# Two graph-attention layers on one core: aggregates scaled on VectorE, weights begun one product sooner, no sums of h in one aggregate

## The chip, the cores and the metric

The kernel runs on one core of a Trainium2 chip. A core has five engines with queues of their own: TensorE (PE in the profile, and PEld for its weight loads), VectorE (DVE), ScalarE (ACT), GpSimd (POOL) and SyncE (SP). Here POOL and SP mostly issue DMA transfers. The metric is the device time of one execution in microseconds. All data is fp32 apart from the masks.

## The reference

There are N = 2708 nodes with 1024 features, and a matrix `adj` of which only `adj > 0` counts. Both layers are residual and work on a normalized input:

```python
h = relu(layernorm(x));  e = relu((h@Wf + bf) @ (h@Wg + bg).T)      # layer l=0
x = x + softmax(where(adj > 0, e, -9e15)) @ (h@W + bW)
h = relu(layernorm(x));  z = h@W1;  e = leaky_relu(z@a1 + (z@a2).T, 0.2)   # layer l=1
x = x + relu(softmax(where(adj > 0, e, -9e15)) @ z)
```

The softmax runs over all nodes for each node, so each layer multiplies a 2708 x 2708 matrix of weights with a 2708 x 1024 matrix. The kernel applies the weights to h first and W afterwards, as softmax(e) @ (h @ W) = (softmax(e) @ h) @ W.

## The kernel before

**Panels.** The nodes for which attention is computed are cut into five panels, p = 0 to 4, of 576, 576, 532, 512 and 512 columns (`width[p]`; h is half of it). The nodes over which the softmax sums are 20 tiles of 128 rows, taken as ten pairs q (NQ = 10), and two left-over tiles, MONO and TINY.

**Products.** Each large product is cut two by two and done with seven products of half size instead of eight (Strassen's scheme in Winograd's form): M1, M5, M2, M6, M7, M3, M4, with sums of operands made beforehand and sums of results made as the products leave PSUM. The tile pool `psum` has eight banks. `accumulate` (line 647) gives four banks to each accumulator: x takes M1 and M2, y takes M5 and M3, z takes M6 and M7, v takes M4. The order in the aggregates that concern us is M1, M5, M2, M6, M3, M7, M4. After a product its four banks are emptied ("evicted"), by DVE or ACT.

**Stages.** In l=0, panel p goes through `scores`, a softmax, `aggregate` (line 885: weights times h) and `project` (line 1202: times W, plus the residual). Around the panel 3 to panel 4 border they interleave; the last two stages of l=0 are the aggregate of panel 4, its fifth, and the projection of panel 4, which goes pair by pair (`by_pair`) and fetches its weight tiles twice. That projection also makes the last rows of h for l=1. In l=1 the scores come from two vectors, so there are only weight steps, `aggregate` for panel 0, `aggregate_quartered` (line 1039) for panels 1 to 4, and a projection after each. In the quartered aggregate each of the seven products is itself done by seven products on quarters (`product`, line 1052), the last of which, `left_out`, is emitted in the next product's time.

**Sums of h.** The quartered aggregates need sums of quarters of h for every product m and every group k of four tiles: 35 steps (`put_quarters`, line 392, tile `hq`). One step is two loads issued by POOL, four DVE instructions of 256 columns, and two stores issued by POOL, 1 MB of traffic in all. They wait in a list `lazy`. From the panel 4 on their buffers come from the pool of slots (54 buffers), two for each step.

**Weight steps of l=1.** `take_shifts(p)` (line 1781) first empties the list `later`, then takes the column maxima (five transposes on PE into two PSUM banks, reductions on DVE) and works out two columns of shifts. `take_weights(p)` (line 1785) spreads them over all partitions (ten transposes on PE) and puts 24 steps at the head of `later`: 22 tiles and two that only lag behind. A step is an ACT instruction, two DVE instructions, an exponential on ACT, and an addition into `sm` on DVE; each has a mask load on SP of its own. `sm` collects the sums by which the aggregate is divided.

**Who is served when.** Between the matmuls the program calls `behind(us)` (line 211). It adds `us` to a credit, capped at twice `us`, and emits work from `later` while the credit is positive, each item at its own price: 2.1 for a weight step, 1.7 for a sum of h. Only where `later` is empty and `spare[0]` is true are items of `lazy` emitted. In an `aggregate` of ten pairs there are four calls per product, three within it and one after its eviction, at a rate of 3.0 in l=0 and 4.0 in l=1. Loads of the next items (`ahead`) are emitted ahead of them. `exps_until` and `quarters_until` emit what must be there, whatever the credit.

**Order on an engine.** What the program emits is a priority, not yet an order: the tile framework's scheduler orders each engine's queue at compile time by when it thinks that an instruction can run and a buffer is free, earlier emitted ones first. [...]

**Scaling.** An aggregate G (two halves `G[0]`, `G[1]`, each of four chunks of columns) is multiplied by the inverse of the sums: `inverse_sums` (line 858) adds `sm` over partitions on PE and takes reciprocals on DVE. In the quartered aggregate the quadrants become final in the order (0,lo) with M2, (1,hi) with M7, (0,hi) with M3 and (1,lo) with M4. `scale` (line 1092) multiplies `G[0]` and the quadrant (1,hi) on POOL after M3, and a DVE instruction at the end multiplies (1,lo). The projection's first product reads `G[0]`.

Of the kernel before, what the change touches and what calls it, by code (L numbers as in the profile page):

```python
# [12 lines left out]
OP = mybir.AluOpType  # L13
# [5 lines left out]
P = 128  # L19
# [6 lines left out]
M1, M5, M6, M7, M3, M2, M4 = range(7)  # L26
# [31 lines left out]
def kernel(  # L58
# [19 lines left out]
    nc = InOrder(tc)  # L78
    N, D = x.shape
    NC = D // P  # L80
    NH = NC // 2
# [3 lines left out]
    NP = N // W  # L85
# [110 lines left out]
    spare, from_slots = [False], [False]  # L196
# [437 lines left out]
    for name, gs in (("pick_lo", (0, 1)), ("pick_hi", (0, 2, 3))):  # L634
        t = consts.tile([P, P], FP, name=name)
# [403 lines left out]
    def aggregate_quartered(p, S, sm, of_right, then={}, fine=1.2):  # L1039

        w = width[p]
        h = w // 2
        hb = h // 2
        lo, hi = slice(0, h), slice(h, w)
        G = both("gT")
        quad = lambda e, s: G[e].rearrange("p (c i) -> p c i", c=NH)[:, :, s]
        make, inner_right = of_right["make"], of_right["right"]
        lasts = {}  # L1050

        def product(m, n, ps, start):
            quarters_until(m)
            if (m, 0) not in lasts:
                for i, of in enumerate((hr_d[:, m, :, :, NK - 1].rearrange("p h f c -> p (h f) c"), hs2_d[:, m, :, NK - 1])):
                    lasts[m, i] = stream("hl2", (P, 4, WH))
                    load(lasts[m, i], of)
            t = stream("hc2", (P, NK - 1, WH))
            raw = n in (M1, M2, M4)
            i = {M1: 0, M2: 1, M4: 3, M6: 0, M3: 1, M7: 2, M5: 3}[n]  # L1060
            load(t, hr_d[:, m, i // 2, i % 2, :NK - 1] if raw else hs2_d[:, m, i, :NK - 1])
            last = lasts[m, int(not raw)][:, i]
            for k in range(NK):
                for d in range(2):
                    lhs = t[:, k] if k < NK - 1 else last
                    nc.tensor.matmul(ps[:, d], lhs[:, d * P:(d + 1) * P], inner_right(m, n, k),  # L1066
                                     start=(start and k == 0 and d == 0), stop=(k == NK - 1), skip_group_check=True)
            behind(fine)

        def bank2(name):  # L1070
            return bank(name)[:, :2 * hb].rearrange("p (d i) -> p d i", d=2)

        def left_over(banks, e, s, fresh):

            two = stream("hl", (P, W + 2 * P))
            load(two, hgl_d[1][:, e])
            cols = lambda b: slice(s.start + b * hb, s.start + (b + 1) * hb)
            for (a, b), ps in banks.items():
                for d in range(2):
                    c = 2 * a + d  # L1080
                    nc.tensor.matmul(ps[:, d], two[:, c * P:(c + 1) * P], S[MONO][:, cols(b)],
                                     start=((a, b) in fresh and d == 0), stop=False, skip_group_check=True)
            for d in range(2):
                for (a, b), ps in banks.items():
                    g = slice(B32 * (2 * a + b), B32 * (2 * a + b) + NY)
                    nc.tensor.matmul(ps[:, d], two[g, W + d * P:W + (d + 1) * P], S[TINY][g, cols(b)], start=False, stop=True,
                                     skip_group_check=True)

        inverse = []
        by = lambda s, c, k: inverse[0][:, s].rearrange("p (o i) -> p o i", o=1).to_broadcast([P, c, k])  # L1090

        def scale():
            for t, s, k in ((quad(0, slice(0, w)), slice(0, w), w), (quad(1, hi), hi, h)):
                nc.gpsimd.tensor_tensor(t, t, by(s, NH, k), OP.mult)

        place = {M1: [(1, lo)], M5: [(0, hi)], M2: [(0, lo)], M6: [(0, hi), (1, lo)], M7: [(1, hi), (1, lo)], M3: [(0, hi)],
                 M4: [(1, lo)]}
        direct = {M1: (0, lo), M5: (0, hi)}
        more_of = {M2: (0, lo), M3: (0, hi), M4: (1, lo)}

        def into_place(m, V, r):
            for e, s in place[m]:
                o = quad(e, s)[:, 2 * r:2 * r + 2]
                if m == M1:
                    nc.scalar.copy(o, V[r])
                elif m == M5:
                    add(o, o, quad(0, lo)[:, 2 * r:2 * r + 2])
                else:
                    add(o, V[r], o)

        def corner():

            four = {(a, b): bank2("gu") for a in range(2) for b in range(2)}
            left_over(four, 1, hi, four)
            for (a, b), ps in four.items():
                at = lambda e: quad(e, slice(h + b * hb, h + (b + 1) * hb))[:, 2 * a:2 * a + 2]
                add(at(1), ps, at(0))

        def with_second():
            exps_until(2 * NQ + 2 + LAG)  # L1120
            make(M2)

        before_next = {M1: lambda: make(M5), M5: with_second, M2: lambda: (of_right["fourth"](), make(M6)), M6: lambda: make(M7),
                       M7: lambda: make(M3), M3: lambda: make(M4)}
        left_out = None
        for m in BY_QUARTERS:
            V = [quad(*direct[m])[:, 2 * r:2 * r + 2] for r in range(2)] if m in direct else [v[:, :, :h] for v in in_pairs("V")]
            c11, c12 = (V[0][:, :, b * hb:(b + 1) * hb] for b in range(2))
            c21, c22 = (V[1][:, :, b * hb:(b + 1) * hb] for b in range(2))
            X = bank2("gx")  # L1130
            product(m, M1, X, True)
            nc.scalar.copy(c21, X)
            if m == M1:
                of_right["fifth"]()
            if left_out:
                left_out()
            Z = bank2("gz")
            product(m, M6, Z, True)
            add(c12, Z, c21)
            Y = bank2("gy")  # L1140
            product(m, M5, Y, True)
            add(c22, Y, c21)
            if m == M7:
                corner()
            if m in before_next:
                before_next[m]()
            product(m, M2, X, False)
            if m not in more_of:
                nc.scalar.copy(c11, X)
            product(m, M7, Z, False)  # L1150
            add(c22, Z, c22)
            product(m, M3, Y, False)
            if m in more_of:
                U = bank2("gu")
                left_over({(0, 0): X, (0, 1): Y, (1, 0): Z, (1, 1): U}, *more_of[m], [(1, 1)])
                nc.scalar.copy(c11, X)
            add(c12, Y, c12)
            if m in more_of:
                add(c22, U, c22)
            into_place(m, V, 0)  # L1160

            def left_out(m=m, V=V, Z=Z, c21=c21):
                product(m, M4, Z, False)
                add(c21, Z, c21)
                into_place(m, V, 1)
                if m == M3:
                    scale()
            if m == M5:
                of_right["second"]()
            if m == M6:  # L1170
                inverse.append(inverse_sums(p, sm))
            if m in then:
                then[m]()
        left_out()
        o = quad(1, lo)
        nc.vector.tensor_tensor(o, o, by(lo, NH, h), OP.mult)
        return [t.rearrange("p (c i) -> p c i", c=NH) for t in G]

    w_in = [w0, w1]
# [486 lines left out]
    for p in range(NP):  # L1666
# [15 lines left out]
        then = {M4: lambda: sums_until(NQ), M5: prepare_W} if p == 0 else {}  # L1682
        ahead[0] = 1 if p == 0 else 2
        if p == NP - 2:
            then[M2] = lambda: first_masks(NP - 1, 0)
            then[M6] = lambda: first_masks(NP - 1, 1)
            then[M7] = lambda: first_masks(NP - 1, 2)
        spare[0], from_slots[0] = p > 0, p == NP - 1
        G[p] = aggregate(0, p, S, got["sm"], then)
        spare[0] = False  # L1690
        if p == 0:
# [89 lines left out]
    def take_shifts(p):  # L1781
        flush()
        got["zm"] = shifts1(p)

    def take_weights(p):
        got["P"] = weights1(p, *got["zm"])
# [3 lines left out]
    for p in range(NP):  # L1790
        S, sm = got["P"]
        then = {}
        if p + 1 < NP:
            then = dict(zip((M2, M6) if p else (M3, M7), (lambda p=p: take_shifts(p + 1), lambda p=p: take_weights(p + 1))))
        spare[0] = p == 0
        g = aggregate_quartered(p, S, sm, next_right, then, fine=1.0) if p else aggregate(1, p, S, sm, then, rate=4.0)
        hooks = {}
        if p + 1 < NP:
            next_right = quarters_of(p + 1, got["P"][0])
            hooks = {M7: next_right["first"]}  # L1800
        project(1, p, g, finish1(p), hooks, by_pair=(p == NP - 1), rate=1.7)
# [29 lines left out]
```

## Time and profile before

| What | Value |
|---|---|
| Median of 14 runs | 3126.07 us (3116.37 to 3129.79) |
| The profiled execution: its time, its span | 3127.64 us, 3125.9 us |
| Granted TensorE clock, mean | 0.984 |
| Busy: PE, DVE, POOL, ACT | 3016.2, 2067.7, 536.3, 463.0 us |
| PE busy in aggregate of panel 4, l=0 (1947 to 2083) | 133.91 of 136 us |
| PE busy in its projection (2083 to 2162) | 56.85 of 79 us, DMA share 1.00 |
| PE busy in aggregate 0 of l=1 (2162 to 2314) | 152 of 152 us |
| PE busy in aggregate 1 of l=1 (2350 to 2520) | 158.60 of 170 us |
| hq instructions on DVE | 28 in 1947 to 2083, 28 in 2162 to 2314 |

A line of the timeline holds the start and the length in us, the engine, the line of the kernel (L45 is the helper through which DVE and ACT instructions are issued), the operation, the tiles written and read, and the number of merged instructions. A bracket at its end is the time that the engine stood idle before it, and what ended the wait. "PEclk" and the granted clock are shares of full speed. "DMA share" is the mean busy share of the 16 DMA engines.

### The profile page before, as it was taken

The page shows a single profiled execution, that of the slowest core. Times are in us where ns is not written, and L with a number is a line of the kernel's source. Part 1 is how long each engine was busy: PE and PEld are TensorE (multiplying, and loading weights), DVE is VectorE, ACT ScalarE, POOL GpSimd, SP SyncE. Part 2 cuts the span into 40 slices and gives each one's busy share as a digit, 9 for nine tenths or more (in the row PEclk, how much of TensorE's full clock was granted, in tenths as well). Part 3 has the DMA queues.
Part 4 walks back from the last instruction along what each step waited for, and adds up shares of the span by engine and source line. Part 5 has one row for each costly group of instructions (what it writes and reads, how often), then busy time and mean ns, then how long its engine had stood idle before and what let it go on. Part 6 is the DMA issues. An engine that isn't in the chain of part 4 may idle for free.

```text
span 3125.9 us, 41677 instructions
## 1 busy us (share of the span) xinstructions
PE 3016.2 (96%) x14630; PEld 2314.1 (74%) x14630; DVE 2067.7 (66%) x4587; ACT 463.0 (15%) x817; POOL 536.3 (17%) x794
## 2 busy tenths in 40 slices
PE   8998999999999999999999999988999999999998
PEld 4576777657877588876888885864767959779694
DVE  5776692776742687527873478657777767777853
ACT  3420020000200101000020002103131121212200
POOL 1421111310112110123111101041211020120202
PEclk9999999999999999999999999998999999999999
DMA  6999967988466796768957677598857768777886
GB/s 230 291 270 257 310 243 261 297 264 243 152 231 161 231 250 211 244 165 254 287 176 249 177 218 246 195 319 291 288 172 246 243 208 298 256 274 272 268 290 247
DMA packets 448576, 764.69 MB, mean 245 GB/s; under 512 B 175776, under 2 KB 262592, under 8 KB 448368
## 3 DMA queue, kind: packets, MB, share of 16 engines
q1 hardware_dynamic: 393008, 598.31, 60.6%
q0 software_dynamic: 55360, 163.73, 15.9%
q8 instruction: 116, 1.90, 0.2%
q14 instruction: 92, 0.75, 0.1%
HBM read 627.95 MB, written 133.91 MB: 244 GB/s over the span
## 4 chain that ended last, share of the span: by engine, by line
PE 70%; DVE 13%; DMA 7%; issue 6%; SPq 2%; POOL 1%; ACT 1%; POOLq 0%; DVEq 0%; ACTq 0%
PE sz L1377 6%; PE gx L661 6%; PE gy L661 6%; PE gz L661 5%; PE gz L1066 5%; PE sx L1377 4%; PE sy L1377 4%; PE pz L1266 4%; PE px L1266 4%; PE py L1266 3%; PE gv L661 3%; PE M_ps L574 3%; PE gy L1066 3%; PE gx L1066 3%; PE qx L661 2%
## 5 line engine op out<-in xcount | busy, mean ns | idle before, releaser
L1377 PE MATMUL sz<-B,As 128*128 128x288 f32 (+2 forms) x1200 | 292.8, 393 | 9.5 <-DVE st L45 8.8
L1377 PEld LDWEIGHTS sz<-B,As 128*128 128x128 f32 x1200 | 228.3, 191 | 59.1 <-DVE st L45 12.7
L1377 PE MATMUL sx<-B,As 128*128 128x288 f32 (+2 forms) x800 | 203.3, 398 | 13.2 <-DMA As<-hs_d 10.1
L1377 PE MATMUL sy<-B,As 128*128 128x288 f32 (+2 forms) x800 | 199.1, 392 | 1.0 <-DMA As<-hs_d 1.0
L661 PE MATMUL gz<-Sa,hc 128*128 128x288 f32 (+2 forms) x800 | 188.1, 396 | 6.0 <-DMA hc<-hg_d 6.0
L1377 PEld LDWEIGHTS sx<-B,As 128*128 128x128 f32 x800 | 153.8, 193 | 47.4 <-issue 6.5
L661 PEld LDWEIGHTS gz<-Sa,hc 128*128 128x128 f32 x800 | 153.3, 192 | 39.0 <-DMA hc<-hg_d 6.4
L1066 PE MATMUL gz<-quarter,hc 128*128 128x128 f32 (+2 forms) x1344 | 170.2, 280 | 6.5 <-DVE gT L45 5.1
L1377 PEld LDWEIGHTS sy<-B,As 128*128 128x128 f32 x800 | 151.9, 190 | 31.7 <-ACT x L45 1.4
L1066 PEld LDWEIGHTS gz<-quarter,hc 128*128 128x128 f32 x1344 | 161.7, 192 | 8.9 <-DVE gT L45 6.5
L1266 PE MATMUL pz<-w,ps 128*128 128x512 f32 x320 | 145.2, 605 | 8.0 <-DVE pt L45 7.0
L1266 PE MATMUL py<-w,ps 128*128 128x512 f32 x320 | 142.5, 595 | 1.9 <-DMA w<-in_L_gnn_W_dram 1.9
L1266 PE MATMUL px<-w,gT 128*128 128x512 f32 x320 | 141.0, 593 | 0.0
L143 POOL DMA_DIRECT2D out_dram<-x_res x180 | 89.0, 500 | 256.6 <-DVE x_res L45 248.2
L143 POOL DMA_DIRECT2D mk_d<-mask x55 | 35.8, 651 | 533.3 <-DVE mask L45 526.9
L1266 PEld LDWEIGHTS pz<-w,ps 128*128 128x128 f32 x320 | 61.3, 194 | 86.9 <-issue 72.2
L1266 PEld LDWEIGHTS py<-w,ps 128*128 128x128 f32 x320 | 60.5, 190 | 77.9 <-issue 72.6
L574 PE MATMUL M_ps<-wgT,wfT 128*128 128x512 f32 x256 | 111.8, 593 | 1.6 <-ACT hsT L45 1.6
L1266 PEld LDWEIGHTS px<-w,gT 128*128 128x128 f32 x320 | 60.3, 190 | 71.0 <-issue 69.0
L661 PE MATMUL gy<-T,hc 128*128 128x288 f32 (+2 forms) x480 | 111.6, 394 | 0.0
L661 PEld LDWEIGHTS gy<-T,hc 128*128 128x128 f32 x480 | 91.4, 190 | 19.3
L977 POOL TENSOR_TENSOR gT<-gT,rr 128x2304 f32<-128x2304 f32 (+5 forms) x12 | 44.4, 3701 | 353.4 <-DVE rr L45 160.9
(378 smaller groups left out, 5864.4 us busy)
## 6 DMA issues: line engine op xcount, KB each, us to landing
hc<-hg_d SPq DMA_DIRECT2D x175, 512.0 KB
As<-hs_d SPq DMA_DIRECT2D x150, 512.0 KB
hc<-hr_d SPq DMA_DIRECT2D x119, 512.0 KB
hc<-hs_d SPq DMA_DIRECT2D x112, 512.0 KB
w<-wt_d SPq DMA_DIRECT2D x96, 512.0 KB
w<-in_L_gnn_W_dram SPq DMA_DIRECT2D x72, 512.0 KB
md<-md_d SPq DMA_DIRECT2D x56, 512.0 KB
adj_i<-in_adj_dram SPq DMA_DIRECT2D x200, 128.0 KB
```

The source lines that it names most:

```text
L143: nc.gpsimd.dma_start(a, b)
L574: nc.tensor.matmul(ps, wfT[a][c // NH][:, c % NH, :], wgT[b][c], start=(c == 0), stop=(c == NC - 1))
L661: nc.tensor.matmul(ps[d], left(m, k, d), right(m, k), start=(start and k == 0), stop=(k == K - 1), skip_group_check=True)
L977: nc.gpsimd.tensor_tensor(of(e, s), of(e, s), by(s, k), OP.mult)
L1066: nc.tensor.matmul(ps[:, d], lhs[:, d * P:(d + 1) * P], inner_right(m, n, k), start=(start and k == 0 and d == 0), stop=(k == NK - 1), ski ...
L1266: nc.tensor.matmul(ps, left[i][m][:, k, :], w_[k], start=(start and k == 0), stop=(k == NH - 1), skip_group_check=True)
L1377: nc.tensor.matmul(ps[:n, :h], lefts[q][:, i % 2, c, :n], B[m][c // 2][:, c % 2, :h], start=(start and c == 0), stop=(c == NH - 1), skip_g ...
```

## The change

1. In the quartered aggregates the scaling moves from POOL to DVE. After each of M2, M7, M3 and M4 the finished quadrant is multiplied in two parts, the first two chunks as soon as they are in place and the other two after the product's `left_out`. For that the inverse of the sums is made after M5 instead of after M6. POOL's two instructions and the single DVE instruction at the end go.
2. In l=1, panel 0, `take_shifts(1)` runs after M6 instead of after M3, and `take_weights(1)` after M3 instead of after M7.
3. In the aggregate of panel 4 of l=0 (the first layer's fifth), `spare[0]` is false, so no sums of h are emitted there. Those that are left come in aggregate 0 of l=1, where `spare[0]` is true as before.

```diff
         inverse = []
-        by = lambda s, c, k: inverse[0][:, s].rearrange("p (o i) -> p o i", o=1).to_broadcast([P, c, k])
-
-        def scale():
-            for t, s, k in ((quad(0, slice(0, w)), slice(0, w), w), (quad(1, hi), hi, h)):
-                nc.gpsimd.tensor_tensor(t, t, by(s, NH, k), OP.mult)
+        done_with = {M2: (0, lo), M7: (1, hi), M3: (0, hi), M4: (1, lo)}
+
+        def scale(m, r):
+            if m in done_with:
+                e, s = done_with[m]
+                o = quad(e, s)[:, 2 * r:2 * r + 2]
+                nc.vector.tensor_tensor(o, o, inverse[0][:, s].rearrange("p (o i) -> p o i", o=1).to_broadcast([P, 2, h]), OP.mult)
...
             into_place(m, V, 0)
+            scale(m, 0)
 
             def left_out(m=m, V=V, Z=Z, c21=c21):
                 product(m, M4, Z, False)
                 add(c21, Z, c21)
                 into_place(m, V, 1)
-                if m == M3:
-                    scale()
+                scale(m, 1)
             if m == M5:
                 of_right["second"]()
-            if m == M6:
+            if m == M5:
                 inverse.append(inverse_sums(p, sm))
             if m in then:
                 then[m]()
         left_out()
-        o = quad(1, lo)
-        nc.vector.tensor_tensor(o, o, by(lo, NH, h), OP.mult)
         return [t.rearrange("p (c i) -> p c i", c=NH) for t in G]
...
-        spare[0], from_slots[0] = p > 0, p == NP - 1
+        spare[0], from_slots[0] = 0 < p < NP - 1, p == NP - 1
         G[p] = aggregate(0, p, S, got["sm"], then)
...
-            then = dict(zip((M2, M6) if p else (M3, M7), (lambda p=p: take_shifts(p + 1), lambda p=p: take_weights(p + 1))))
+            then = dict(zip((M2, M6) if p else (M6, M3), (lambda p=p: take_shifts(p + 1), lambda p=p: take_weights(p + 1))))
```

## The prediction

> **What bounds the kernel now.** I read the page's shares first, then the table of stretches over the end of layer l=0 and layer l=1, then the timeline wherever TensorE (PE) stands still in it.
>
> ```profile
> PE 3016.2 (96%) x14630; PEld 2314.1 (74%) x14630; DVE 2067.7 (66%) x4587; ACT 463.0 (15%) x817; POOL 536.3 (17%) x794
> ```
>
> PE is busy for 96% of 3125.9 us, so the change can only pay in the 110 us where PE is idle or slowed. The stretches say where these lie (columns: stretch, length, busy us with instructions of PE, PE's weight loads, VectorE (DVE), ScalarE (ACT), GpSimd (POOL); then granted clock, share of the DMA engines, GB/s):
>
> ```profile
> 1947.00:2083.00 136.00, 133.91 (x635) 114.86 (x633) 95.58 (x208) 13.85 (x25) 33.81 (x39) 1.00 0.73 248
> 2083.00:2162.00 79.00, 56.85 (x132) 25.05 (x130) 47.74 (x120) 10.77 (x19) 21.84 (x31) 0.84 1.00 337
> 2162.00:2314.00 152.00, 152.00 (x645) 117.05 (x646) 117.33 (x216) 41.32 (x69) 27.98 (x30) 0.99 0.69 226
> 2314.00:2350.00 36.00, 36.00 (x86) 15.93 (x85) 30.30 (x45) 13.43 (x21) 5.96 (x12) 1.00 0.63 191
> 2350.00:2520.00 170.00, 158.60 (x1164) 146.29 (x1163) 124.42 (x315) 30.49 (x57) 18.17 (x22) 0.95 0.74 252
> 2578.00:2712.00 134.00, 128.85 (x1126) 126.37 (x1125) 103.68 (x276) 23.08 (x43) 12.17 (x12) 0.97 0.81 279
> ```
>
> These are: the fifth aggregate of l=0, its projection, aggregate 0 of l=1, its projection, and aggregates 1 and 2 of l=1. The projection loses 22 us and has the DMA engines full. Aggregate 1 loses 11.4 us where aggregate 2 loses 5.2. Aggregate 0 loses nothing.
>
> In the first two stretches the timeline shows (bracket: PE's idle time before it, and what ended it):
>
> ```profile
> 2061.88 14.32 PE L661 MATMUL gv<-Sb,hc 128*128 128x256 f32 x64 [2.09 <-DVE m L45]
> 2103.28 5.12 PE L1266 MATMUL pz<-w,ps 128*128 128x512 f32 x8 [6.97 <-DVE pt L45]
> 2108.24 3.60 PE L1266 MATMUL py<-w,ps 128*128 128x512 f32 x8
> 2132.07 2.37 PE L1266 MATMUL py<-w,ps 128*128 128x512 f32 x4 [1.90 <-DMA w<-in_L_gnn_W_dram]
> ```
>
> The first wait stands behind sums of h (tile hq): DVE sat waiting for their loads before it could empty the banks. The second is DVE waiting until 2098.89 for the residual rows, whose bias loads POOL issued at 2083.16 to 2092, after its 28 hq loads and stores. The eight matmuls after it took 5.12 us instead of 3.60. Behind 2135 lies a serial tail (statistics, dots, shifts; PE waits 8.3 and 3.8 us) that the change doesn't touch.
>
> Aggregate 0 of l=1 on DVE, and where PE needs it next:
>
> ```profile
> 2239.43 0.43 DVE L45 TENSOR_TENSOR hq<-hq 128x256 f32<-128x256 f32 x1 [5.46 <-DMA hq<-hr_d]
> 2253.80 0.43 DVE L45 TENSOR_TENSOR hq<-hq 128x256 f32<-128x256 f32 x1 [2.64 <-DMA hq<-hr_d]
> 2255.52 1.54 DVE L45 TENSOR_TENSOR u<-gz,m 128x288 f32<-128x288 f32 x4
> 2263.12 0.46 DVE L45 TENSOR_TENSOR gT<-gy,u 128x288 f32<-128x288 f32 x1 [6.05 <-PE gy L661]
> ```
>
> Seven hq steps end at 2255.6; the last four came 5.8 us apart, each waiting for its loads. The eviction of M6 (u) queues behind them and comes 12 us after PE ended M6 at 2243.6; PE wants those banks only at 2267.35. The eviction of M3 (gT) is on time, and PE's `sum_ps` follows at 2265.83.
>
> The start of aggregate 1:
>
> ```profile
> 2374.33 4.21 PE L1066 MATMUL gx<-P,hc 128*128 128x144 f32 x16 [5.32 <-ACT gT L45]
> 2380.81 2.23 PE L1066 MATMUL gz<-quarter,hc 128*128 128x144 f32 x16 [1.37 <-DVE gT L45]
> ```
>
> DVE and ACT are still making the last weight steps there; an ACT copy that frees a bank queues behind their exponentials.
>
> The scaling (L1094) on POOL, in aggregate 2:
>
> ```profile
> 2672.70 2.85 POOL L1094 TENSOR_TENSOR gT<-gT,rr 128x1064 f32<-128x1064 f32 x1 [85.34 <-DVE gT L45]
> ```
> ```profile
> 2669.45 0.68 DVE L45 TENSOR_TENSOR sm<-sm,P 128x512 f32<-128x512 f32 x1
> ...
> 2673.15 2.94 DVE L45 TENSOR_TENSOR sm<-sm,P 128x512 f32<-128x512 f32 x1
> ```
>
> The same DVE instruction takes 0.68 us alone and 2.94 us under the POOL one.
>
> [...] after 5.32 us idle, 16 matmuls took 4.21 us, later ones 2.12. [...] SP's weight loads for the projection took 13.7 to 18.8 us each in the chain while the share was 1.00. [...]
>
> **The change, part by part.** The sums are against the profiled execution, 3127.64 us (span 3125.9 and 1.7 around it); the median of the runs is 1.57 lower.
>
> *Scaling.* Out, per aggregate 1 to 4: two POOL instructions and one DVE instruction (1.36, 1.27, 1.23, 1.23 us). In: eight DVE instructions of 576, 532, 512, 512 elements. DVE instructions of these sizes take 0.76, 0.71, 0.69 us (gT<-V,gT)[...]. That adds 4.7+4.4+4.3+4.3 = 17.7 us of DVE. The locks that go: 2.4 (aggregate 1), 2.3+3.5 (2), 2.2+3.4 (3) = 13.8 us. Aggregates 1 to 3 each have one PE wait of 3.3 us (gz L1081 on DVE V), some 10 us after a lock of 2.3, with DVE busy in between. Against it stand two quarters of M7, 1.5 us: 0.8 gained, three times. The sums' inversion (four matmuls, two reciprocals of 1.8 to 1.95 us) moves from after M6 to after M5. Its operand was final about 15 us before; DVE had waits of 3.1 and 1.2 us just after M5 in aggregate 2, and the banks that queue behind it are wanted two products (4.6 us) later. I take 0. The last scaling lies under the projection's first product (6.9 us; 3.4 in the last panel). Sum: -2 (from -6, all three waits shrinking by the lock, to +4, the reciprocals or quarters late in front of an eviction).
>
> *Weights sooner in aggregate 0.* By the credit rule (4 us per call, four calls per product, 2.1 us per step), the 24 weight steps of panel 1 now fall as 10 in M4, 11 in the projection, 3 in aggregate 1. The timeline has 10, 10 and 2 of its 22 real ones there. After: 10 in M7, 8 in M4, 6 in the projection, none left. With them move 22 mask loads on SP; 11 were issued at 2252 to 2267 already, ahead of the projection's loads, so they cost nothing more while SP keeps that lead. At stake in aggregate 1: 5.3+1.4 waits, 2.1 slow clock and 0.4 more = 9.2 us. But `take_shifts` needs two PSUM banks where y and z hold all eight, so its five transposes (0.7 us) can't start before M3's first eviction, as now. Their chain ended at 2276.25, 9 us into M7, and the ten spreading transposes need it: 0 if they are placed within M7, 9 us lost if directly after M3. And DVE has to be free at 2276. I take -6 (from -9 to +9).
>
> *No sums in the fifth aggregate.* Seven hq steps leave 2047 to 2083: 28 DVE instructions (13.6 us), 28 POOL issues (20.2 us), 7 MB. From 2047 to 2132 the DMA engines moved about 28.3 MB; 21.3 MB in 70 us is 304 GB/s, under the 337 to 417 seen there. So 2.1+0.9 (a weight load)+7.0+1.5 (the slow clock) = 11.5 us should go; the last wait, 1.9 and 1.3 of clock, I leave, since weights are still fetched as slots come free. Bounds: 14.7 and 0.
>
> They go to aggregate 0 of l=1: 14 steps instead of 7, by the credits one at the end of M2, seven before M6's eviction, two after, four before M3's. From 2255.6 on each takes 3.2 us (four POOL issues of 0.72) to 5.8 us. M6's eviction behind eight steps comes at about 2260: no loss. M3's, behind n steps, comes at 2255.6+(n-7)x4.0, and behind it wait `sum_ps`, the transposes and M7. The scheduler puts an eviction that is ready before a step whose loads aren't, so n is 9 to 14; I take 12: 2275.6 against 2265.8 = +10 (0 at n=9; 23 at n=14 and 4.7 us).
>
> Sum: -2-6-11.5+10 = -9.5: 3118.1 in the profiled execution's terms, 3116.6 as a median.
>
> **The rivals.** *Clean*: n is 9 or less and DVE keeps up: -2-9.2-14.7 = -26: 3100. For it: aggregates 1 to 3 of l=0 take seven steps each without a PE wait. Against it: their loads were there beforehand; here the slots free up only at 2207. *Given back*: n=13 at 4.3 us makes 15.6 us, DVE's lateness leaves 2 of the 9 at aggregate 1: -2-2-11.5+15.6 = 0: 3126. *Slower*: n=14 at 4.7 us: PE stands 23 us at `sum_ps`, the weights start later than now, nothing is won in aggregate 1, scaling 0: +11.5: 3138, more if the spreads wait too. It decides where M3's eviction comes over 15 us late. For it: the 12 us by which M6's eviction was late already. *Not moved*: the scheduler fetches the seven early as before, into the fifth aggregate: -2-6 = -8: 3118. Against it: masks and residuals now come first for the slots.
>
> **How the numbers follow.** Likeliest 0.40, clean 0.12, not moved 0.05, given back 0.19, slower 0.24. The likeliest alone: 3110 to 3120. All: 3102 to 3138, leaving out most of clean and half of slower. 0.2% is 6.3 us, about what a measurement of this kernel can tell from no change: faster 0.57, same 0.19, slower 0.24.
>
> **What would show it.** Right: no hq before about 2160; bias loads on POOL some 10 us sooner and the 6.97 us wait gone; 14 hq steps in aggregate 0; the 5.32 us wait gone; no POOL work from aggregate 1 on but DMA issues and memsets. Wrong: M3's eviction or `sum_ps` over 15 us late, a PE wait on `sp_ps`, or the projection of panel 4 as long as before because weights, not residuals, are what is late.

## The result and the profile after

The changed kernel takes 3108.76 us in the median of 10 runs (3105.11 to 3113.63), the kernel before 3124.95 us in the median of all its runs by then. The ratio is 0.9951, with a 95% interval of 0.9942 to 0.9960: 15 us faster (13 to 18). The profiled execution took 3110.9 us with a span of 3109.1 us, 16.8 us under the span before.

The page's shares after:

```profile
PE 3004.3 (97%) x14630; PEld 2306.6 (74%) x14630; DVE 2068.2 (67%) x4615; ACT 463.3 (15%) x817; POOL 505.2 (16%) x786
```

PE does the same 14630 instructions in 12 us less busy time (3016.2 before): some of its matmuls run faster than they did, and the last lines of this section show sixteen of them. By stages, from the first matmul of each stage to that of the next, in the two profiled executions:

| Stage | before, us | after, us | difference |
|---|---|---|---|
| all that comes ahead of the fifth aggregate | 1947.4 | 1948.9 | +1.5 |
| l=0, fifth aggregate and its projection | 214.6 | 199.1 | -15.5 |
| l=1, aggregate 0 | 151.5 | 174.9 | +23.4 |
| projection 0 | 48.1 | 48.9 | +0.8 |
| aggregate 1 | 154.7 | 140.2 | -14.5 |
| aggregate 2 | 133.8 | 127.4 | -6.4 |
| aggregate 3 | 131.1 | 125.0 | -6.1 |
| aggregate 4, projections 1 to 4 | unchanged | unchanged | 0 |

The table of stretches after, for the same stages as before (the last is aggregate 2; columns as before):

```profile
1948.00:2084.00 136.00, 136.00 (x641) 116.28 (x640) 85.52 (x183) 13.97 (x26) 20.61 (x19) 1.00 0.71 225
2084.00:2148.00 64.00, 50.97 (x127) 23.30 (x125) 45.99 (x118) 10.79 (x19) 14.58 (x22) 0.88 0.98 351
2148.00:2300.00 152.00, 131.04 (x547) 100.42 (x547) 119.07 (x226) 40.22 (x68) 45.69 (x57) 0.93 0.74 238
...
2359.00:2515.00 156.00, 153.81 (x1165) 142.70 (x1165) 115.92 (x307) 25.23 (x47) 9.87 (x21) 0.98 0.80 273
2567.00:2701.00 134.00, 131.33 (x1140) 125.77 (x1139) 108.77 (x303) 24.98 (x46) 7.35 (x17) 1.00 0.86 295
```

The fifth aggregate is now full (136.00 of 136), and its projection is 13 us shorter (67.0 us instead of 79.9). Aggregate 0 of l=1, which lost nothing before, loses 21 us and has a clock of 0.93 (the stretch leaves out its last 23 us). Aggregates 1 and 2 have gone from 0.95 and 0.97 of full clock to 0.98 and 1.00.

The timeline of PE after, in the projection and its tail, in aggregate 0 and in aggregate 2:

```profile
2095.68 3.70 PE L1266 MATMUL pz<-w,ps 128*128 128x512 f32 x8 [0.78 <-DVE pt L45]
2138.62 1.33 PE L849 MATMUL mx_ps<-ident,mx 128*128 128x128 f32 x5 [8.34 <-DVE mx L45]
...
2270.08 1.11 PE L849 MATMUL mx_ps<-ident,mx 128*128 128x128 f32 x4 [20.03 <-DVE gT L45]
2300.51 15.79 PE L661 MATMUL gv<-P,hc 128*128 128x288 f32 x64 [1.45 <-DVE m L45]
...
2678.45 0.72 PE L1081 MATMUL gz<-P,hl 128*128 128x133 f32 x4 [1.19 <-DVE V L45]
2680.22 2.08 PE L1066 MATMUL gx<-T,hc 128*128 128x133 f32 x16
```

The wait of 6.97 us in the projection is down to 0.78, and the 1.90 us wait for a weight load is gone too; the serial tail (8.34) is as it was. The 20.03 us are new. DVE's timeline shows what they stand behind:

```profile
2265.12 0.43 DVE L45 TENSOR_TENSOR hq<-hq 128x256 f32<-128x256 f32 x1 [6.92 <-DMA hq<-hr_d]
...
2269.23 0.42 DVE L45 TENSOR_TENSOR hq<-hq 128x256 f32<-128x256 f32 x1
2269.57 0.81 DVE L45 TENSOR_TENSOR gT<-gy,u 128x288 f32<-128x288 f32 x2
```

All fourteen sums stand ahead of M3's eviction (`gT<-gy,u`) in DVE's queue, and DVE is idle for 6.92 us ahead of one of the last, waiting for its loads. The first sum started at 2213.80: 55.8 us for fourteen, 4.0 us each. PE wants the banks at 2250.05 for the transposes of `take_shifts`, which now come inside M3. M3's first two banks were complete then, as PE stood still from there on, and yet their eviction started only at 2269.57, behind the last sum: DVE worked through its queue in the order given to it.

The last two PE lines above are to be set against the same place of aggregate 2 in the kernel before:

```profile
2685.63 0.72 PE L1081 MATMUL gz<-P,hl 128*128 128x133 f32 x4 [3.28 <-DVE V L45]
2688.16 3.92 PE L1066 MATMUL gx<-T,hc 128*128 128x133 f32 x16
```

The wait has fallen from 3.28 to 1.19 us, and the 16 matmuls after it from 3.92 to 2.08 us. PE's busy time in this aggregate falls by 3.5 to 4 us, its idle time by 2.5: the slower matmuls behind the wait had cost more than the wait itself gives back.

### The profile page after: what moved, and what is told of

It reads as the page before. It is cut to its first block, busy times and chain, and to the rows that moved or that the text cites. A ratio compares the mean times of both kernels' runs of the same rounds, so it can differ in the third digit from the quotient of the medians.

```text
span 3109.1 us, 41683 instructions
## 1 busy us (share of the span) xinstructions
PE 3004.3 (97%) x14630; PEld 2306.6 (74%) x14630; DVE 2068.2 (67%) x4615; ACT 463.3 (15%) x817; POOL 505.2 (16%) x786
## 4 chain that ended last, share of the span: by engine, by line
PE 71%; DVE 13%; issue 7%; DMA 6%; POOL 2%; SPq 1%; ACT 1%; POOLq 0%; DVEq 0%; ACTq 0%
PE sz L1377 7%; PE gz L661 6%; PE gz L1066 5%; PE gy L661 5%; PE gx L661 5%; PE sx L1377 4%; PE sy L1377 4%; PE pz L1266 4%; PE px L1266 4%; PE py L1266 3%; PE M_ps L574 3%; PE gx L1066 3%; PE gy L1066 3%; PE qz L661 3%; PE gv L661 2%
```

## The experiments

The runs were made on several chips, the kernel before beside them each time; its median there was 3129 to 3131 us, so ratios are compared, not times. Ahead of the fifth aggregate, where no edit changes the work, the profiled executions differ by up to 8 us (it starts between 1947.4 and 1955.6 us); so single stages are compared in them, not spans. The projection of panel 4 varies too where sums stay in the fifth aggregate (75.7 us in weights_alone, 78.9 to 79.9 in the other three), so what part 3 gains there is known to a few us only.

### Each part alone

```diff
 scaling_alone: the kernel before, with
+scale(m, 0) ... scale(m, 1) on VectorE;  inverse_sums after M5      (part 1)
 weights_alone: the kernel before, with
+then = dict(zip((M2, M6) if p else (M6, M3), ...                    (part 2)
 no_sums_alone: the kernel before, with
+spare[0], from_slots[0] = 0 < p < NP - 1, p == NP - 1               (part 3)
 without_no_sums: the changed kernel, with
-spare[0], from_slots[0] = 0 < p < NP - 1, p == NP - 1
+spare[0], from_slots[0] = p > 0, p == NP - 1                        (parts 1 and 2)
```

> The kernel before with the scaling on VectorE and the inversion after M5, nothing else. Theory (the prediction left out the half clock): each PE wait of 3.3 us at M4 of aggregates 1 to 3 falls to between 1 and 2.2 us, and [...] the 16 matmuls after it take 2.0 to 2.1 us instead of 3.8 to 4.2: -13 us in all (-10 to -17). Rival (the prediction's step): only the waits shrink, by 0.8 each: -2 us, and not under -6; then most of the 17 us that the two traces show there would come from the other parts.

> The kernel before with the shifts after M6 and the weights after M3, nothing else. Theory: seven sums of h end at about 2255, as before, so M3's eviction and the transposes of the shifts (mx_ps) come with less than 2 us of PE wait, and the waits of 5.3 and 1.4 us at the start of aggregate 1 go: -9 us. Rival: the transposes, now inside M3, themselves hold PE for over 10 us whatever the number of sums: 0 or slower.

> The kernel before without sums of h in the fifth aggregate, nothing else. Theory: the fifth aggregate and its projection give 15 us, and the fourteen sums in aggregate 0 of l=1 cost about 20 us of PE wait, now at sum_ps or M7, as the shifts are not yet there: between 0 and +10 us, +5 the middle. Rival: the 20 us wait after the change belongs to the shifts standing inside M3, and fourteen sums alone cost under 5 us: -10 to -15 us.

> The changed kernel with sums of h allowed in the fifth aggregate again (parts 1 and 2 alone). Theory: part 3 gives 15.5 us upstream and takes 23.6 in aggregate 0, so without it the kernel is some 8 us faster than the changed one: 3100 us, -24 against the kernel before. Rival: the wait in aggregate 0 comes with part 2 as much as with part 3, and part 3 pays: 3115 us or more.

| Kernel | ratio to before | 95% interval | us of 3131 |
|---|---|---|---|
| scaling_alone | 0.9949 | 0.9935 to 0.9963 | -16 |
| weights_alone | 0.9973 | 0.9962 to 0.9983 | -8 |
| no_sums_alone | 1.0036 | 1.0025 to 1.0046 | +11 |
| without_no_sums | 0.9909 | 0.9893 to 0.9925 | -28 |

The scaling alone gives as much as the whole change. Its three aggregates take 151.3, 127.4 and 125.0 us against 154.7, 133.8 and 131.1 before. The timeline of PE in scaling_alone, aggregate 2:

```profile
2685.93 0.72 PE L1081 MATMUL gz<-P,hl 128*128 128x133 f32 x4 [1.20 <-DVE V L45]
2687.70 2.08 PE L1066 MATMUL gx<-T,hc 128*128 128x133 f32 x16
```

That is the picture of the changed kernel, without the other two parts. The weights alone do what they should: aggregate 1 takes 143.5 us instead of 154.7, aggregate 0 loses 3.2 (1.45 of it a wait of PE ahead of M4, at `gv`, which the changed kernel has too) and its projection 0.8. With seven sums the transposes of `take_shifts` inside M3 wait for nothing; it isn't their place that makes the stall. The sums alone are a loss, 1 us above the expected range. The wait is there, at `sum_ps`, as the transposes come later in that kernel (timeline of PE in no_sums_alone):

```profile
2278.71 2.29 PE L864 MATMUL sum_ps<-sm,ones 128*128 128x288 f32 x4 [21.17 <-DVE gT L45]
```

So part 3 gains 14 to 15.5 us in the fifth aggregate and its projection and pays 21 to 25 back in aggregate 0, whichever way the weights are placed. In the profiled executions the changed kernel also takes 3.3 us more in aggregate 1 than without_no_sums (140.2 against 137.0): both have a wait of 2.2 us there, and slow matmuls behind it only the changed kernel (the last section comes back to this). Without part 3 the kernel is 13 us faster than the changed one; the intervals don't touch.

### Why the fourteen sums are slow

Two readings were open: POOL issues the loads of the next sums only behind the stores of the last (a ring of load, sum and store), or the DMA engines can't bring so much. Three kernels separate them and try remedies. (In three_in_the_fifth three of the seven sums are held back and four stay.)

```diff
 loads_deeper: the changed kernel, with
-        for it in of[:ahead[0]]:
+        for it in of[:5 if of is lazy and from_slots[0] else ahead[0]]:
 five_in_aggregate_1: the changed kernel, with
-            credit[0] -= one(lazy)
+            credit[0] -= one(lazy) * (4.5 / 1.7 if from_slots[0] else 1.0)
...
-        spare[0] = p == 0
+        spare[0] = p <= 1
 three_in_the_fifth: the changed kernel, with part 3 undone, and in the fifth aggregate
-        while spare[0] and not later and lazy and credit[0] > 0:
+        while spare[0] and not later and len(lazy) > keep[0] and credit[0] > 0:
...
+        keep[0] = 7 - 3 if p == NP - 1 else 0
```

> The changed kernel with the loads of five sums of h issued ahead instead of two, in aggregate 0 of l=1 alone; all fourteen sums still stand ahead of M3's eviction on VectorE. Theory (the steps are slow because the next loads stand behind the last stores in POOL's queue, a ring of load, sum and store): a step falls from about 4.0 to about 3 us, which is its four issues on POOL, the last sum ends near 2255, and PE's wait of 20 us falls to under 8: -12 us or more against the changed kernel, ratio to the kernel before about 0.991. Rival (the DMA engines can't bring 14 MB beside the products' own loads any faster): the wait stays at 15 us or more, or turns into waits of PE for hc: ratio 0.994 or more.

> The changed kernel with sums of h dearer in aggregate 0 of l=1 (so nine of the fourteen stand ahead of M3's eviction) and allowed in aggregate 1, where the other five go. Theory (the 20 us wait is the queue of sums ahead of the eviction): nine sums end at about 2247 to 2252, PE waits under 4 us at mx_ps, and aggregate 1, without a PE wait over 2.2 us and with 46 us of idle VectorE, takes five sums for 0 to 8 us: -12 to -20 us against the changed kernel, ratio to the kernel before 0.989 to 0.991. Rival: the sums cost in aggregate 1 what they save in aggregate 0, as a product there can start only with its sums stored and loaded again: ratio 0.994 or more.

> The changed kernel with four of the seven sums of h left in the fifth aggregate's time (three are held back, so eleven fall to aggregate 0 of l=1; by the queue's order four stand ahead of M7's eviction in the fifth aggregate, ten ahead of M3's in aggregate 0). Theory: both ends are in proportion to the steps: ten steps end near 2254, so the wait at mx_ps falls from 20 us to 3 to 6, and of the 15.5 us gained upstream about half stays: between the changed kernel and parts 1 and 2 alone or a little below both, ratio 0.990 (0.988 to 0.993). Rival: the first sums in the fifth aggregate cost the whole 15 us, as the bias loads come late behind any of them: ratio 0.994 or more.

| Kernel | ratio to before | 95% interval | aggregate 0, us |
|---|---|---|---|
| changed kernel | 0.9951 | 0.9942 to 0.9960 | 174.9 |
| loads_deeper | 0.9894 | 0.9879 to 0.9909 | 157.8 |
| five_in_aggregate_1 | 0.9889 | 0.9871 to 0.9907 | 155.8 |
| three_in_the_fifth | 0.9908 | 0.9893 to 0.9923 | 158.4 |

For the tile hq, the answer on its DMA issues in the changed kernel has, as what POOL (first line) and DVE (second) sat waiting for (us, times):

```profile
  DVE hq L45: 32.8, 10
  DMA hq<-hr_d: 28.9, 10
```

and in loads_deeper:

```profile
  DVE hq L45: 14.7, 4
  DMA hq<-hr_d: 11.7, 10
...
DMA to landing us min/median/max: 4.1/6.1/8.6
```

In the changed kernel POOL waits for DVE to finish a sum before it can store it, DVE waits for loads that POOL has not issued yet, and each waits some 30 us for the other. With five loads ahead both waits fall below half, though each transfer now takes longer to land (median 6.1 us, 4.7 before that). The fourteen sums take 38.7 us, 2.8 each instead of 4.0. That is about what POOL needs to issue the four transfers of a step (0.73 each). PE's wait is 2.85 us in loads_deeper and 2.06 in five_in_aggregate_1, where nine sums stand ahead of the eviction (timelines of PE, loads_deeper first):

```profile
2259.62 1.12 PE L849 MATMUL mx_ps<-ident,mx 128*128 128x128 f32 x4 [2.85 <-DVE gT L45]
```
```profile
2256.70 0.66 PE L849 MATMUL mx_ps<-ident,mx 128*128 128x128 f32 x4 [2.06 <-DVE gT L45]
```

The ring theory holds, and the bandwidth rival falls for the changed kernel: during its fourteen sums the DMA engines have a share of 0.86 and 283 GB/s, and with five loads ahead they bring 362 GB/s. Their share is 1.02 then, so little room is left; which of POOL's issues and the DMA engines now sets the 2.8 us was not tested. The five sums moved to aggregate 1 cost nothing there: it takes 140.2 us, as in the changed kernel. In three_in_the_fifth the trace has four sums in the fifth aggregate's time and ten in aggregate 0. The loss in aggregate 0 is small, as expected, but the fifth aggregate and its projection take 204.1 us against 199.1, and its ratio is that of parts 1 and 2 alone.

The last kernel has both remedies:

```diff
 deeper_and_later: the changed kernel, with the edits of loads_deeper and of five_in_aggregate_1
```

> Both remedies together: five sums' loads ahead, and the sums dearer in aggregate 0 of l=1 with the rest allowed in aggregate 1. By the queue's order twelve stand ahead of M3's eviction and two go to aggregate 1. Theory (each removes the same wait, so they don't add): PE's wait at mx_ps under 2 us and the time within 5 us of the two remedies alone, ratio 0.988 to 0.990. Rival (deeper loads also relieve the DMA engines' later work): 0.986 or less.

The ratio is 0.9865, interval 0.9848 to 0.9881: 42 us faster than the kernel before and some 27 faster than the changed one. That is better than I expected, and near the rival's figure; but the interval overlaps those of both single remedies. No wait of PE over 1.2 us is left in aggregate 0, which takes 152.8 us against 157.8 and 155.8 with one remedy: each remedy alone left a wait of 2 to 3 us, slow matmuls behind it (the clock is 0.98 in that stage), and in loads_deeper also the 1.45 us ahead of M4. That is 3 to 5 us of the 8 to 13 between the profiled executions, and another 1.6 lie in aggregate 1. The remaining 3 to 6 us lie ahead of the fifth aggregate, where the profiles differ whatever was changed; why was not looked into, and how much of the lead over each single remedy is owed to it stays open.

### What the scaling on POOL cost

The scaling's gain was eight times what I had put down. Three kernels look for its cause inside the changed kernel.

```diff
 longer_wait: the changed kernel, with
             product(m, M7, Z, False)
+            if m == M4:
+                for _ in range(5):
+                    add(junk[:, :2 * hb].rearrange("p (d i) -> p d i", d=2), Z, c22)
             add(c22, Z, c22)
 longer_wait_in_M3: the same with "if m == M3:"
 pool_beside: the changed kernel, at the end of scale(m, r), with
+            if m == M7 and r == 1:
+                of = quad(1, hi)
+                nc.gpsimd.tensor_tensor(beside[...], of, inverse[0][:, hi] ..., OP.mult)
```

> The changed kernel with five further VectorE additions of 256 to 288 columns (0.4 us each, results not used) ahead of the eviction of gz after M7 inside M4 of each quartered aggregate, so that PE's wait there grows by about 2 us, from 2.2, 1.2, 1.2 and less. Theory (a wait near 3.3 us brings the half clock with it): in aggregates 2 and 3, where it is not there now, the 16 matmuls after the wait go from 2.0 to about 3.8 us and some 0.4 more follow, so each loses about 4 us, aggregate 1 about 2, aggregate 4 between 0 and 4: +10 to +14 against the changed kernel. Rival (the clock drops for another reason, and only the waits grow): +6 to +8.

> The changed kernel with the five additions of longer_wait moved to where PE's wait is: ahead of the eviction of gz after M7 inside M3 (not M4), 0.4 us each, results not used. In longer_wait they stood in M4, where nothing waited for them, so it told nothing of the clock. Theory (a wait near 3.3 us brings the half clock with it): the waits of 2.2, 1.2, 1.2 us grow to about 4.2, 3.2, 3.2; in aggregates 2 and 3 the first 16 matmuls of M4 go from 2.0 to about 3.8 us, so each loses 4 us or more, aggregate 1 about 2 to 4, aggregate 4 under 2: +10 to +14 against the changed kernel, ratio to the kernel before 0.998 to 0.9996. Rival (only the waits grow): +6, ratio 0.997.

> The changed kernel with a POOL multiplication in each quartered aggregate after M7's last part: the quadrant (1,hi) times the inverse into a scratch tile that nobody reads, as many elements as in the kernel before. Theory [...]: a VectorE instruction with two SBUF operands is stretched by 2.2 to 2.5 us in each aggregate, PE's waits at M3 in aggregates 1 to 3 come back to about 3.3 us and the half clock behind them: +10 to +15 against the changed kernel, ratio 0.998 to 1.000. Rival (it was the order on VectorE, the inversion after M6 or the weight steps, and not POOL): under +3, ratio 0.995 to 0.996.

longer_wait was a miss of mine: PE's wait is at the end of M3, not in M4. Its ratio, 0.9942 (0.9926 to 0.9959), is that of the changed kernel, so 2 us of DVE work four times in M4 cost nothing. In the right place the same additions gave 0.9998 (0.9989 to 1.0006): 15 us, the whole gain of the change. PE's timeline of longer_wait_in_M3, aggregate 2:

```profile
2686.22 1.09 PE L1081 MATMUL gz<-P,hl 128*128 128x133 f32 x4 [3.99 <-DVE V L45]
2688.44 3.91 PE L1066 MATMUL gx<-T,hc 128*128 128x133 f32 x16
```

The waits grew by 2.5, 2.8 and 2.8 us to 4.64, 3.99 and 3.92. That is 8 us. The three aggregates take 2.2, 6.0 and 5.9 us longer than in the changed kernel, 14.1 in all: in aggregate 1, where the matmuls behind the wait were slow already, about the wait alone; in 2 and 3, where the 16 matmuls behind are now slow too (3.91 us instead of 2.08 in aggregate 2), twice the wait.

pool_beside gave 0.9992 (0.9983 to 1.0001), 13 us over the changed kernel. In its aggregate 2, on POOL, on DVE and on PE (lines of the kernel are one higher here):

```profile
2675.85 2.44 POOL L1100 TENSOR_TENSOR beside<-gT,rr 128x1064 bf16<-128x1064 f32 x1 [85.46 <-DVE gT L45]
```
```profile
2676.03 2.63 DVE L45 TENSOR_TENSOR quarter<-T 128x133 f32<-128x133 f32 x2
```
```profile
2687.91 1.25 PE L1082 MATMUL gz<-P,hl 128*128 128x133 f32 x4 [3.32 <-DVE V L45]
2691.18 3.48 PE L1067 MATMUL gx<-T,hc 128*128 128x133 f32 x16
```

Two small DVE instructions that take 0.50 us in the changed kernel take 2.63 under the POOL instruction; the 2.1 us come out 10 us later as PE's wait, 3.32 instead of 1.19, and the 16 matmuls after it take 3.48 us instead of 2.08. Aggregates 1 to 3 take 3.1, 5.0 and 5.2 us longer: that is what a POOL instruction of 2.4 to 3 us costs that nobody waits for. The inversion after M5 and the eight multiplications on DVE are in both kernels, so the POOL instruction by itself is enough to take back 13 of the 16 us. It doesn't follow that the inversion's move was worth nothing: a wait can be brought to 3.3 us by more than one thing, and no kernel has the scaling on DVE with the inversion left after M6. The next section says what the traces show of it.

## Why the prediction was right, and where it was wrong

The time fell within the range and on the forecast's side, 7 us below the figure in the profiled executions (-16.8 against -9.5), and a little below the range of the likeliest path alone. The four terms were less good than their sum:

- **Scaling: -2 put down, -16 measured (scaling_alone).** That a DVE instruction held up under POOL's (2.94 us against 0.68 in aggregate 2; the prediction calls it a lock) ends as a PE wait of 3.3 us ten us later was right, and pool_beside shows it. Two terms were mis-sized. First, I priced the wait alone. The slow clock that I had read behind the 5.32 us wait (16 matmuls in 4.21 us, later ones in 2.12) stood behind these three as well: 4.21, 3.92 and 3.78 us for 16 matmuls in aggregates 1 to 3. It was worth 3.5 to 4 us in aggregate 2, more than the wait gave back. Second, the inversion's move was put at 0. DVE's timeline in aggregate 2 shows otherwise, first before, then after:

```profile
2647.85 1.81 DVE L45 RECIPROCAL rr<-sum_ps 128x266 f32<-128x266 f32 x1
...
2654.82 0.43 DVE L45 TENSOR_TENSOR V<-gz,V 128x266 f32<-128x266 f32 x1
```
```profile
2648.77 0.44 DVE L45 TENSOR_TENSOR V<-gz,V 128x266 f32<-128x266 f32 x1 [0.30 <-PE gz L1066]
```

The `V<-gz` line is the same eviction in both kernels, early in M7. PE starts the product that it empties 72.6 us into the stage in both kernels. After, DVE waits for PE here, 75.1 us into the stage; before, it comes later, at 76.8, with the two reciprocals of 1.8 us shortly ahead in its queue. From here to the late eviction that PE waits for, DVE has no pause but one of 0.69 us for ACT in both kernels, and it takes 29.2 us instead of 30.3. That is the 2.3 us of the hold-up less the two quarters, about the 0.8 that I had. So this eviction comes 2.9 us sooner, and by my reckoning 1.8 of it is the inversion's. PE's wait falls by 2.1 in aggregates 2 and 3 and by 1.1 in aggregate 1. How the 16 us divide between hold-up and inversion no run shows.

- **Weights sooner: -6 put down, -7 to -8 measured.** Right in kind, with both sides larger. Aggregate 1 gains 11.2 us in weights_alone, not the 9.2 at stake; aggregate 0 and its projection give 4.0 back. The transposes of the shifts did fit into M3.
- **No sums in the fifth aggregate: -11.5 put down, -14 to -15.5 measured.** The bias loads on POOL came at 2064 instead of 2083, and DVE was on time, as said. "The last wait, 1.9 and 1.3 of clock, I leave" was the part that was wrong: it went as well, with the DMA engines at 351 GB/s in that stretch.
- **The sums in aggregate 0: +10 put down, +21 to +25 measured.** "The scheduler puts an eviction that is ready before a step whose loads aren't, so n is 9 to 14; I take 12" failed: n was 14. M6's eviction was interleaved with the sums, M3's was not. With n = 14 the formula puts M3's eviction at 2283.6. Measured, it started at 2269.57 in a stage that began 14.0 us sooner, which is the same place, and 17.8 us behind the 2265.8 that it was set against. But two errors cancel in that: the first seven steps ended 4.4 us sooner than I took, and the last seven took 4.6 us each, not 4.0. (Two readings behind the rate were off as well: four issues of 0.72 make 2.9 us, not 3.2, and the last four steps of the kernel before started 4.8 us apart on average, not 5.8.) PE's wait is longer than the delay, 20.0 us, since the change had moved the transposes of `take_shifts` ahead of `sum_ps`, and PE stands at them. With 2.1 of slow clock and the 1.45 at `gv`, which belongs to part 2, it makes up the stage's +23.4.
- **The rival "slower"** had this stall right, n = 14 at 4.7 us, and its consequences wrong: the weights began 132.8 us into the stage (132.1 before), and the start of aggregate 1 was clean. Its "scaling 0" was mis-sized in the same way as my -2.

An eviction of M3 that is over 15 us late stood on the list of what would show the prediction wrong, and it came 17.8 us late by that measure. So the path was wrong there, and the time came out within the range by luck: the scaling brought 14 us more than put down, the other two gains together 3 to 6 more, and the sums in aggregate 0 cost 11 to 15 more. The sign was safe for a reason that I didn't have: the scaling alone outweighs all that part 3 loses. What the prediction calls a lock stands in the runs as a delay: two DVE instructions take 2.63 us under POOL's in pool_beside and 0.50 in the changed kernel. Not every one is delayed: in the kernel before, at 2697.74, `V<-gz,V`, which reads gz from PSUM, took 0.43 us under a POOL instruction of 5.01. What makes the difference was not tested.

## What to carry to other kernels

A wait of PE of some 3 us cost about double in this kernel, since the matmuls behind it took nearly twice as long (16 of them 3.92 us instead of 2.08 in aggregate 2); price the clock at every wait near that length, and look for the small work on another engine, 10 us earlier, that made it. Where an engine is busy without a break, count what leaves the stretch as well as what comes in. Where work is pushed out of one stage, count it in the queue where it lands, all of it, ahead of whatever that queue has to do on time. Where two engines each show long waits for the other around one buffer, as POOL and DVE did over hq, issue loads further ahead before deciding that bandwidth is short.

## What the runs showed of the hardware

In these runs no one length of PE's wait parts slow matmuls from fast ones. Waits of 1.15 to 1.20 us at the end of M3 in aggregates 2 and 3 never slowed the 16 matmuls after them (2.05 to 2.08 us, in the eight kernels whose waits there are that long). Waits of 3.2 to 4.6 us did so every time (3.39 to 4.21 us). A wait of 2.2 us in aggregate 1 mostly did (3.39 to 4.21 us in seven kernels) but not in without_no_sums, where the same wait of 2.19 us was followed by 2.23 us. What tells these two apart was not found.
